# A selective-scan decoder layer on one core: products of B two units ahead in three buffers, a softplus factor in a shared tile

## The chip, the cores and the metric

The kernel runs on one core of one Trainium2 chip. A core has PE (TensorE, matrix products), DVE (VectorE), ACT (ScalarE), POOL (GpSimd) and SP (SyncE, which here only issues DMAs); each runs its own queue of instructions in order and waits on semaphores for the others. The metric is device microseconds of one execution. Before the change the median of 7 runs is 1651.39 us (1644.49 to 1654.64).

## The reference

The layer takes x of shape (4, 512, 512), four batches of 512 tokens, and adds three blocks in turn, each behind a layer norm.

1. A selective state-space block (Mamba), with 1024 channels and 16 states. Cut to what matters:

```
delta = softplus(dt_proj(dt) + bias)
h     = h * exp(delta * A) + (delta * u) * B      # for every token in turn, channel and state
y     = sum over the states of h * C
out   = out_proj((y + u * D) * silu(z))
```

2. An expert-like block with two "smooth-quantised" int8 products per batch.
3. A mixture of 16 experts with the two best chosen per token, and a shared expert.

## The kernel before

**Units.** The recurrence is done for one batch after the other. A batch has 8 chunks `c` of 128 channels; a chunk has 8 units `n`. A unit holds 2 x 32 channels with 4 of the 16 states on 128 partitions, over 512 tokens: a tile of 128 x 1024. There are 4 x 8 x 8 = 256 units. In this text scans and products are counted 0 to 255 over all batches, and chunks 0 to 31. A unit takes these steps:

- decays, two ScalarE exponentials `da` (L724) into PSUM, two buffers;
- the product of B, `bu` = B row x (delta u), on POOL (L726), two buffers in SBUF;
- the scan `da = scan(da, bu)` on VectorE (L733), which runs the recurrence along the tokens in place;
- the output `h` = da x C row on VectorE (L739);
- after four units, PE sums the states into the bank `py` (L751, `state_sums`).

**What a unit needs.** `delta(b, c)` makes a chunk's softplus: one PE product (L668), activations on ScalarE (L680 to L693: absolute value, relu, exponential, 1 + e in a tile `sp_w`, that less 1, and the logarithm in place in `sp_w`, with a table load), then on POOL a subtraction, two additions and a product with u (L695 to L701) and a memset of the first column (L703). The result is the tile `dd` (delta and delta u), two buffers. `spread(b, c, p)` then copies half a chunk's `dd` to all state rows by two DMAs on SP (L711), into `rep`, three buffers: units 0, 1, 4, 5 of a chunk read its half `p` = 0, units 2, 3, 6, 7 its half `p` = 1. The rows of B and C, `bc`, are loaded per batch in four groups (`scan_bc`, L656), one buffer each.

**The order of the work.** Nothing is reordered later: what the Python program writes is the order in each queue. `scan_batch` writes, for each unit: the decays and the product of the *next* unit (`unit_inputs`), state sums where due, other work, the scan, other work, the output, then the copies and loads that are due, other work. The "other work" (`more`) is taken from generators, one step at a time: softplus chains of coming chunks (`deltas`), the projections, convolution and gates of the next batch (`fronts`), and the second and third block of the batch before with the first group of experts (`backs`, `routed`). A generator yields what its next step needs, and `Pace` holds a running estimate of when each engine and tile will be free. A step is written if no engine it uses is estimated more than `BEHIND` later than VectorE, and its inputs no more than `SLACK`. For POOL these are 500 and -300 ns.

A half's spread is queued in `copies` (half 1 of the next chunk at unit 5, half 0 of the chunk behind it at unit 7) and written when its softplus is estimated ready. Where it isn't, it is forced, its chain's steps written out at once: half 0 after unit 6, half 1 after unit 7 of the chunk before. The B and C rows of the next batch are loaded in the last chunk after unit 4 (groups 0 and 1) and unit 7 (groups 2 and 3).

**The tail.** After the last scan come the back part of batch 3 (projection L806, quantised products, routing), what is left of the first group's expert tiles (steps L1505 to L1561: an indirect load of tokens and one of weights by POOL, transposes L400, products L1538 and L1553), then the second group of experts and the weighted sums (L1301, L1311).

Of the kernel before, what the change touches and what calls it, by code (L numbers as in the profile page):

```python
# [8 lines left out]
F32 = mybir.dt.float32  # L9
BF16 = mybir.dt.bfloat16  # L10
F16 = mybir.dt.float16
U32 = mybir.dt.uint32
# [7 lines left out]
P = 128  # L20
B = 4
L = 512
DM = 512
NT = L // P
NK = DM // P
DI = 1024
NC = DI // P
# [105 lines left out]
class Pace:  # L133
# [6 lines left out]
    TABLES = {"Exp": 0, "Tanh": 0, "Silu": 1, "Ln": 2}  # L140


    SLACK = {"DVE": 200, "Activation": 700, "Pool": -300, "PE": 3500, "SP": 500}
    BEHIND = {"DVE": 0, "Activation": 1500, "Pool": 500, "PE": 5000, "SP": 4000}

    def __init__(self, nc):
        self.nc, self.seen, self.table, self.queue = nc, 0, None, 0
# [95 lines left out]
def following(b, c, n):  # L243

    return (b, c + n) if c + n < NC else (b + 1, c + n - NC)
# [24 lines left out]
class Kernel:  # L270
# [388 lines left out]
    def delta(self, b, c):  # L659

        nc, sb, st = self.nc, self.sb, self.state[b]
        Z = self.bank

        first = (b, c) == (0, 0)
        ew, EW = (nc.vector, None) if first else (nc.gpsimd, POOL)
        yield PE, Z.free, lambda: "dt" in st and all(k >= (b, c) or x.over for k, x in self.deltas.items())
        pd = Z.take([P, L])
        nc.tensor.matmul(pd, self.wdt_sb[:, c * P : (c + 1) * P], st["dt"], start=True, stop=True)  # L668
        if c == NC - 1:
            del st["dt"]  # L670

        bias = self.bdt_sb[:, c : c + 1]
        e = sb.tile([P, L], F32, name="sp_e", bufs=1)
        w = sb.tile([P, L], F32, name="sp_w", bufs=1)
        r = sb.tile([P, L], F32, name="sp_r", bufs=1)
        dd = sb.tile([P, 2, L], F32, name="dd", bufs=2)
        st["dd", c] = dd
        delta, du = dd[:, 0, :], dd[:, 1, :]
        yield ACT, pd
        nc.scalar.activation(e, pd, AF.Abs, bias=bias)  # L680
        nc.scalar.activation(r, pd, AF.Relu, bias=bias)  # L681
        Z.done(pd)
        yield ACT
        nc.scalar.activation(e, e, AF.Exp, scale=-1.0)
        nc.scalar.activation(w, e, AF.Copy, bias=1.0)
        yield ACT
        if first:
            nc.vector.tensor_scalar_add(du, w, -1.0)
        else:
            nc.scalar.activation(du, w, AF.Copy, bias=-1.0)  # L690
        yield ACT, self.no_table
        self.table = True
        nc.scalar.activation(w, w, AF.Ln)  # L693
        yield du, EW
        ew.tensor_sub(e, e, du)  # L695
        yield EW
        ew.tensor_add(e, e, r)
        yield w, EW
        ew.tensor_add(delta, e, w)
        yield EW  # L700
        ew.tensor_mul(du, delta, st["u"][c])  # L701

        ew.memset(delta[:, 0:1], STOP)  # L703
# [9 lines left out]
            )  # L713
        st["rep"][c, p] = rep

    def unit_inputs(self, b, c, n):

        nc, st = self.nc, self.state[b]
        g, p = UNITS[n]
        rep = st["rep"][c, p]  # L720
        da = self.pscan.tile([P, NP, L], F32, name="da", bufs=2)
        for i in range(NP):
            q = c * NQC + p * NP + i
            nc.scalar.activation(da[:, i, :], rep[:, i, 0, :], AF.Exp, scale=self.a_sb[:, q, g : g + 1])  # L724
        bu = self.sb.tile([P, NP, L], F32, name="bu", bufs=2)
        nc.gpsimd.tensor_mul(bu, st["bc"][0, g].unsqueeze(1).to_broadcast([P, NP, L]), rep[:, :, 1, :])  # L726
        st["da"][c, n], st["bu"][c, n] = da, bu

    def unit_scan(self, b, c, n):
        st = self.state[b]  # L730
# [459 lines left out]
    def route(self, sb, G, b, xnT, gate):  # L1190

        nc = self.nc
        yield PE, xnT, gate, G.free
        pl = G.take([P, NT, P])
        for t in range(NT):
            for k in range(NK):
                nc.tensor.matmul(
                    pl[:, t, : E + 1],
                    xnT[:, k, t * P : (t + 1) * P],
                    gate[:, k, :],  # L1200
                    start=(k == 0),
                    stop=(k == NK - 1),
                )
        yield pl
        lg = pl[:, :, : E + 1]

        m = sb.tile([P, NT], F32, name="rt_m")
        nc.vector.tensor_reduce(m, lg[:, :, :E], AX.X, ALU.max, negate=True)
        p = sb.tile([P, NT, E + 1], F32, name="rt_p")
        nc.vector.tensor_add(p[:, :, :E], lg[:, :, :E], m.unsqueeze(2).to_broadcast([P, NT, E]))  # L1210
        nc.vector.tensor_scalar(p[:, :, E], lg[:, :, E], -1.0, 80.0, ALU.mult, ALU.min)
        yield ACT, p
        nc.scalar.activation(lg, p, AF.Exp)
        yield pl
        sg = sb.tile([P, NT], F32, name="sg")
        nc.vector.tensor_scalar_add(sg, lg[:, :, E], 1.0)
        nc.vector.reciprocal(sg, sg)
        nc.vector.tensor_reduce(m, lg[:, :, :E], AX.X, ALU.add)
        nc.vector.reciprocal(m, m)
        nc.vector.tensor_mul(p[:, :, :E], lg[:, :, :E], m.unsqueeze(2).to_broadcast([P, NT, E]))  # L1220
        G.done(pl)

        top = sb.tile([P, NT, 8], F32, name="rt_top")
        idx = sb.tile([P, NT, 8], U32, name="rt_idx")
        for t in range(NT):
            nc.vector.max(top[:, t, :], p[:, t, :E])
            nc.vector.max_index(idx[:, t, :], top[:, t, :], p[:, t, :E])
            if t % 2:
                yield
        nc.vector.tensor_copy(self.idf[:, b * NT : (b + 1) * NT, :], idx[:, :, 0:2])  # L1230
        nc.vector.tensor_reduce(m, top[:, :, 0:2], AX.X, ALU.add)
        nc.vector.reciprocal(m, m)
        yield POOL, m
        nc.gpsimd.tensor_mul(
            self.topw[:, b * NT : (b + 1) * NT, :], top[:, :, 0:2], m.unsqueeze(2).to_broadcast([P, NT, 2])
        )
        self.done.add(("route", b))
        return sg
# [115 lines left out]
    def sort(self, sb, G, group, fixed, pos, tok, wrow, count, first_weights, few):  # L1354
# [29 lines left out]
        nc.vector.tensor_copy(tot, pr[:, 1].rearrange("p t e -> p e t"))  # L1384
        G.done(pr)

        run = sb.tile([P, E, T], F32, name="run", bufs=1)
        nc.vector.tensor_tensor_scan(
            run.rearrange("p e t -> p (e t)"),
            keep.rearrange("p e t -> p (e t)"),  # L1390
# [194 lines left out]
    def run(self, ctx):  # L1585
# [21 lines left out]
        with tc.tile_pool(name="front", bufs=2) as fsb:  # L1607
            self.fsb = fsb
            self.first = ExitStack()
            sb = self.first.enter_context(tc.tile_pool(name="first", bufs=1))  # L1610
            self.xnT0 = sb.tile([P, NK, L], F32, name="xnT0", bufs=1)
            self.bank.add(self.pscan, "py")
            self.first_front(sb, self.bank)
            self.bank.names.remove((self.pscan, "py"))
            self.deltas, self.copies = {}, []
            for c in range(2):
                self.steps_of(0, c)
                self.skip(0, c)
            self.end(self.deltas[0, 0])
            self.spread(0, 0, 0)  # L1620
            for g in range(2, NG):
                self.scan_bc(0, g)
            self.spread(0, 0, 1)
            self.copies.append((0, 1, 0))
            self.fronts = Steps(self.pace, (w for b in range(1, B) for w in self.front(b)))
            self.unit_inputs(0, 0, 0)
            pool = ctx.enter_context(ExitStack())
            routed = Steps(self.pace, self.first_experts())
            backs = Steps(self.pace, self.backs(pool))
            backs.due = lambda slot: BACK_STEPS * (slot - NC * NU) / DUE  # L1630
            self.fronts.due = lambda slot: FRONT_STEPS * slot / DUE
            self.scan_batch(0, [Steps(self.pace, self.first_gates(sb))])
            for b in range(1, B - 1):
                self.scan_batch(b, [backs])
            assert self.fronts.over
# [59 lines left out]
    def scan_batch(self, b, beside):  # L1695

        self.started.add(b)
        for i in range(NC * NU):
# [3 lines left out]

            nb, nc = following(b, c, (n + 1) // NU)
            if nb < B:
                self.unit_inputs(nb, nc, (n + 1) % NU)

            if n == 4:
                self.state_sums(b, c, 0)
# [14 lines left out]
            if n == 5:  # L1723
                self.skip(*following(b, c, 2))
                self.copies.append((*following(b, c, 1), 1))
            if n == 7:
                self.copies.append((*following(b, c, 2), 0))
            while self.copies:
                db, dc, p = self.copies[0]
                if db < B:  # L1730
                    late = (db, dc) == following(b, c, 1) and n == NU - 2 + p or (db, dc) == (b, c)
                    if late:
                        self.end(self.deltas[db, dc], [*self.deltas.values(), self.fronts, *beside])
                    elif not self.deltas[db, dc].over or self.pace.ready(self.state[db]["dd", dc]) > self.pace.engine["DVE"]:
                        break
                    self.spread(db, dc, p)
                self.copies.pop(0)
            if b + 1 < B and c == NC - 1 and n in (4, 7):
                for g in range(2):
                    self.scan_bc(b + 1, g + (n == 7) * 2)  # L1740
            self.more(beside, 0)
# [67 lines left out]
```

## Time and profile before

| | |
|---|---|
| median of 7 runs | 1651.39 us |
| the profiled execution | 1649.16 us |
| span of its instructions | 1647.4 us |
| busy: PE, VectorE, POOL, ScalarE | 1199.6, 1196.7, 1126.6, 941.0 us |
| granted PE clock, mean | 0.853 |
| first scan to end of last | 85.6 to 1326.5 us |
| before the first scan; after the last | 85.6; 320.9 us |

Busy time is time in which an engine executes. The page's groups put instructions of one line together: line, engine, operation, what it writes and reads, count, then busy time in all, mean nanoseconds of one, and the idle time of that engine just ahead of them with what ended most of it. The answers on waits give total, number and longest. `PEld` is PE loading weights; `DVE da L733` is the scan's tile by the line that wrote it.

### The profile page before, as it was taken

To read this page: it belongs to the slowest core of one execution; us is meant where nothing else is said; L and a number is where in the kernel's file an instruction comes from. 1 tells how busy PE (TensorE), PEld (TensorE's weight loads), DVE (VectorE), ACT (ScalarE), POOL (GpSimd) and SP (SyncE) were. 2 spreads that over 40 slices of the span, in tenths; PEclk is the share of its full clock that TensorE was granted. 3 is DMA by queue.
4 is the path that set the end of the run, shared out by engine and by line. 5 is a ranking of instruction groups with operands and counts; after the bars stand their busy time and mean duration, and the time that the engine had idled before them with its cause. 6 is when DMAs were issued, how large, how long until landed. Compare 5 with 4: busy or idle time off the path is not lost. (4 is left out here: it accounts for less than half of the span.)

```text
span 1647.4 us, 15732 instructions
## 1 busy us (share of the span) xinstructions
PE 1199.6 (73%) x4552; PEld 586.7 (36%) x4552; DVE 1196.7 (73%) x1256; ACT 941.0 (57%) x1592; POOL 1126.6 (68%) x935
## 2 busy tenths in 40 slices
PE   5867877557866767898778885865666899668980
PEld 2223222112332323333423432353424447444760
DVE  4488999989867888878878898877787935453212
ACT  3386776755758779546787752667675415510330
POOL 1078899887768888667887874777787544135454
PEclk9978988778887887998988897888777999869995
DMA  6466555575244546665434768654567474268956
GB/s 203 143 177 137 130 117 110 125 187 111 78 89 93 124 125 178 163 190 132 98 85 118 175 149 277 164 143 124 145 178 200 122 263 146 87 254 277 338 195 217
DMA packets 109658, 262.22 MB, mean 159 GB/s; under 512 B 16192, under 2 KB 20416, under 8 KB 109504
## 3 DMA queue, kind: packets, MB, share of 16 engines
q1 hardware_dynamic: 93120, 204.50, 47.6%
q0 software_dynamic: 16448, 56.65, 9.9%
q8 instruction: 40, 0.66, 0.2%
q14 instruction: 50, 0.41, 0.1%
HBM read 168.55 MB, written 45.88 MB: 130 GB/s over the span
## 5 line engine op out<-in xcount | busy, mean ns | idle before, releaser
L726 POOL TENSOR_TENSOR bu<-bc,rep 128x1024 f32<-128x1024 f32 x256 | 602.6, 2360 | 178.7 <-DVE da L733 137.9
L733 DVE TENSOR_TENSOR_SCAN da<-da,bu 128x1024 f32<-128x1024 f32 x256 | 586.2, 2290 | 88.0 <-POOL bu L726 54.8
L724 ACT ACTIVATE da<-rep,a_sb 128x512 f32<-128x512 f32 x512 | 352.6, 690 | 250.7 <-DVE h L739 223.1
L739 DVE TENSOR_TENSOR h<-da,bc 128x1024 f32<-128x1024 f32 x256 | 312.1, 1219 | 18.5 <-PE py L751 8.2
L751 PE MATMUL py<-h,sel 128*32 128x512 f32 x1024 | 162.8, 677 | 45.6 <-DVE h L739 45.6
L1263 POOL DMA_INDIRECT wx<-in_wexp,wrow x62 | 63.5, 1025 | 87.4 <-PE bank L1553 35.4
L502 POOL TENSOR_TENSOR u<-u,tap 128x511 f32<-128x511 f32 (+2 forms) x72 | 91.3, 1268 | 16.2 <-ACT tap L498 13.9
L446 PE MATMUL bank_a<-xnT,win 128*128 128x512 f32 x176 | 93.4, 680 | 8.4 <-ACT tap L498 5.6
L446 PE MATMUL bank_g<-xnT,win 128*128 128x512 f32 x184 | 90.2, 636 | 7.6 <-ACT tap L498 4.2
L751 PEld LDWEIGHTS py<-h,sel 128*32 128x32 f32 x1024 | 31.8, 117 | 155.0 <-issue 81.0
L1507 POOL DMA_INDIRECT xs<-xn_d,tok x62 | 64.5, 1041 | 20.6 <-issue 17.7
L446 PE MATMUL bank_b<-xnT,win 128*128 128x512 f32 x120 | 60.8, 653 | 12.9 <-ACT sp_r L681 10.8
L446 PEld LDWEIGHTS bank_a<-xnT,win 128*128 128x128 f32 x176 | 37.9, 223 | 59.2 <-issue 47.9
L446 PEld LDWEIGHTS bank_g<-xnT,win 128*128 128x128 f32 x184 | 36.3, 205 | 59.9 <-issue 43.8
L411 DVE SCALAR_TENSOR_TENSOR hs<-hs,bank 128x128 f32<-128x128 f32 x24 | 6.8, 285 | 64.8 <-ACT hs L1544 48.7
L1538 PE MATMUL bank<-xT,wx 128*128 128x128 f32 x384 | 48.4, 283 | 1.9 <-ACT xT L1529 1.4
L695 POOL TENSOR_TENSOR sp_e<-sp_e,dd 128x512 f32<-128x512 f32 x31 | 39.5, 1274 | 14.3 <-ACT dd L690 14.1
L1301 POOL DMA_INDIRECT yg<-y_d,pos x32 | 32.7, 1023 | 24.0 <-DMA y_d<-ys 9.7
L1538 PEld LDWEIGHTS bank<-xT,wx 128*128 128x128 f32 x384 | 46.3, 198 | 5.4 <-issue 3.3
L1311 DVE SCALAR_TENSOR_TENSOR xr<-yg,topw,xr 128x512 f32<-128x512 f32 x32 | 23.6, 749 | 29.6 <-DMA yg<-y_d,pos 29.2
L806 PE MATMUL bank_g<-wout,u 128*128 128x512 f32 x64 | 34.6, 699 | 11.1 <-ACT tap L498 6.2
L446 PEld LDWEIGHTS bank_b<-xnT,win 128*128 128x128 f32 x120 | 24.7, 213 | 48.5 <-issue 30.3
(434 smaller groups left out, 2407.4 us busy)
## 6 DMA issues: line engine op xcount, KB each, us to landing
rep<-dd SPq DMA_DIRECT2D x128, 512.0 KB
win<-in_win SPq DMA_DIRECT2D x64, 256.0 KB
x<-xr SPq DMA_DIRECT2D x48, 256.0 KB
xr<-x SPq DMA_DIRECT2D x48, 256.0 KB
y_d<-ys SPq DMA_DIRECT2D x48, 256.0 KB
bc<-rows_d SPq DMA_DIRECT2D x32, 256.0 KB
gz_d<-gz SPq DMA_DIRECT2D x32, 256.0 KB
gzl<-gz_d SPq DMA_DIRECT2D x32, 256.0 KB
```

Source lines behind the costliest of these rows:

```text
L446: nc.tensor.matmul(pj, win[:, k, :], xnT[:, k, :], start=(k == 0), stop=(k == NK - 1))
L502: nc.gpsimd.tensor_add(u[:, j:], u[:, j:], v[j][:, j:])
L695: ew.tensor_sub(e, e, du)
L724: nc.scalar.activation(da[:, i, :], rep[:, i, 0, :], AF.Exp, scale=self.a_sb[:, q, g : g + 1])
L726: nc.gpsimd.tensor_mul(bu, st["bc"][0, g].unsqueeze(1).to_broadcast([P, NP, L]), rep[:, :, 1, :])
L733: self.nc.vector.tensor_tensor_scan(daf, daf, buf, 0.0, ALU.mult, ALU.add)
L739: self.nc.vector.tensor_mul(h, st["da"].pop((c, n)), st["bc"][1, g].unsqueeze(1).to_broadcast([P, NP, L]))
L751: nc.tensor.matmul(py[q * CH : (q + 1) * CH, :], self.sel, st["h"][c, g, q // NP][:, q % NP, :], start=False, stop=(g == NG - 1),)
L806: nc.tensor.matmul(po[t], st["u"][c][:, t * P : (t + 1) * P], wout[c], start=(c == part[0]), stop=(c == part[-1]),)
L1263: nc.gpsimd.indirect_dma_start(out=ws[s], out_offset=None, in_=self.wexp, in_offset=bass.IndirectOffsetOnAxis(ap=wrow[:, s : s + 1], axis= ...
L1507: nc.gpsimd.indirect_dma_start(out=xs[s], out_offset=None, in_=xn_d, in_offset=bass.IndirectOffsetOnAxis(ap=tok[:, s : s + 1], axis=0), bo ...
L1538: nc.tensor.matmul(ph[:, i, :], w[:, o : o + P], xT[:, k, :], start=(k == 0), stop=(k == NK - 1))
```

## The change

The product is taken out of `unit_inputs` and made two units ahead, with a third `bu` buffer; the decays stay one unit ahead. `sp_w` is gone: 1 + e and its logarithm now stand in the delta half of `dd`, and the steps that follow wait for `dd`. POOL's `SLACK` goes to 2500 and its `BEHIND` to 3500. Half 0 is queued at unit 6 instead of 7 and forced after unit 5 instead of 6; half 1 as before. Groups 0 and 1 of the next batch's rows are loaded after unit 3 instead of 4. Some tiles of the routing have one buffer, and the experts' sort runs its scan in place in `keep`. The packs of state sums are as they were.

```diff
-    SLACK = {"DVE": 200, "Activation": 700, "Pool": -300, "PE": 3500, "SP": 500}
-    BEHIND = {"DVE": 0, "Activation": 1500, "Pool": 500, "PE": 5000, "SP": 4000}
+    SLACK = {"DVE": 200, "Activation": 700, "Pool": 2500, "PE": 3500, "SP": 500}
+    BEHIND = {"DVE": 0, "Activation": 1500, "Pool": 3500, "PE": 5000, "SP": 4000}
...
-        w = sb.tile([P, L], F32, name="sp_w", bufs=1)
...
+        w = delta
...
-        yield du, EW
+        yield dd, EW
         ew.tensor_sub(e, e, du)
         yield EW
         ew.tensor_add(e, e, r)
-        yield w, EW
+        yield dd, EW
         ew.tensor_add(delta, e, w)
...
-    def unit_inputs(self, b, c, n):
+    def unit_decays(self, b, c, n):
...
-        bu = self.sb.tile([P, NP, L], F32, name="bu", bufs=2)
-        nc.gpsimd.tensor_mul(bu, st["bc"][0, g].unsqueeze(1).to_broadcast([P, NP, L]), rep[:, :, 1, :])
-        st["da"][c, n], st["bu"][c, n] = da, bu
+        st["da"][c, n] = da
+
+    def unit_products(self, b, c, n):
+
+        nc, st = self.nc, self.state[b]
+        g, p = UNITS[n]
+        bu = self.sb.tile([P, NP, L], F32, name="bu", bufs=3)
+        nc.gpsimd.tensor_mul(
+            bu, st["bc"][0, g].unsqueeze(1).to_broadcast([P, NP, L]), st["rep"][c, p][:, :, 1, :]
+        )
+        st["bu"][c, n] = bu
...
-        run = sb.tile([P, E, T], F32, name="run", bufs=1)
+        run = keep
...
-            self.unit_inputs(0, 0, 0)
+            self.unit_decays(0, 0, 0)
+            for n in range(2):
+                self.unit_products(0, 0, n)
...
             if nb < B:
-                self.unit_inputs(nb, nc, (n + 1) % NU)
+                self.unit_decays(nb, nc, (n + 1) % NU)
+            nb, nc = following(b, c, (n + 2) // NU)
+            if nb < B:
+                self.unit_products(nb, nc, (n + 2) % NU)
...
-            if n == 7:
+            if n == 6:
                 self.copies.append((*following(b, c, 2), 0))
...
-                    late = (db, dc) == following(b, c, 1) and n == NU - 2 + p or (db, dc) == (b, c)
+                    late = (db, dc) == following(b, c, 1) and n == NU - 3 + 2 * p or (db, dc) == (b, c)
...
-            if b + 1 < B and c == NC - 1 and n in (4, 7):
+            if b + 1 < B and c == NC - 1 and n in (3, 7):
+                while ("rows", b + 1) not in self.done:
+                    self.fronts.go()
```

The tiles `rt_m`, `rt_p`, `sg`, `rt_top` and `rt_idx` of the routing get `bufs=1`.

More of the change, by code (lines that the diff above doesn't have):

```diff
@@ L1205, in route @@
         lg = pl[:, :, : E + 1]
-        m = sb.tile([P, NT], F32, name="rt_m")
+        m = sb.tile([P, NT], F32, name="rt_m", bufs=1)
         nc.vector.tensor_reduce(m, lg[:, :, :E], AX.X, ALU.max, negate=True)
-        p = sb.tile([P, NT, E + 1], F32, name="rt_p")
+        p = sb.tile([P, NT, E + 1], F32, name="rt_p", bufs=1)
         nc.vector.tensor_add(p[:, :, :E], lg[:, :, :E], m.unsqueeze(2).to_broadcast([P, NT, E]))
@@ L1214, in route @@
         yield pl
-        sg = sb.tile([P, NT], F32, name="sg")
+        sg = sb.tile([P, NT], F32, name="sg", bufs=1)
         nc.vector.tensor_scalar_add(sg, lg[:, :, E], 1.0)
@@ L1221, in route @@
         G.done(pl)
-        top = sb.tile([P, NT, 8], F32, name="rt_top")
-        idx = sb.tile([P, NT, 8], U32, name="rt_idx")
+        top = sb.tile([P, NT, 8], F32, name="rt_top", bufs=1)
+        idx = sb.tile([P, NT, 8], U32, name="rt_idx", bufs=1)
         for t in range(NT):
```

## The prediction

> **What bounds the kernel now.** I read the page's groups first, then the waits of VectorE and POOL, then the busy time by stage, then the timeline of one long wait. The page's four costliest groups: the product, the scan, the decays and the output of a unit.
> ```profile
> L726 POOL TENSOR_TENSOR bu<-bc,rep 128x1024 f32<-128x1024 f32 x256 | 602.6, 2360 | 178.7 <-DVE da L733 137.9
> L733 DVE TENSOR_TENSOR_SCAN da<-da,bu 128x1024 f32<-128x1024 f32 x256 | 586.2, 2290 | 88.0 <-POOL bu L726 54.8
> L724 ACT ACTIVATE da<-rep,a_sb 128x512 f32<-128x512 f32 x512 | 352.6, 690 | 250.7 <-DVE h L739 223.1
> L739 DVE TENSOR_TENSOR h<-da,bc 128x1024 f32<-128x1024 f32 x256 | 312.1, 1219 | 18.5 <-PE py L751 8.2
> ```
> A unit costs VectorE 2.29 + 1.22 = 3.51 us, POOL 2.36, ScalarE 2 x 0.69. ScalarE and POOL mostly stand waiting for VectorE (223.1 and 137.9 us): VectorE sets the pace. Busy time by stage (batch 0, 1, 2, 3 of the scans; the first part of the tail; the rest of it):
> ```profile
> core 0: us, PE busy (x) PEld busy (x) DVE busy (x) ACT busy (x) POOL busy (x), PEclk, DMA share, GB/s
> 85.60:348.10 262.50, 180.48 (x524) 62.21 (x524) 238.50 (x160) 193.07 (x304) 234.75 (x166) 0.81 0.59 131
> 348.10:663.50 315.40, 222.53 (x788) 99.35 (x788) 260.99 (x234) 225.47 (x379) 252.29 (x202) 0.84 0.51 125
> 663.50:987.40 323.90, 268.21 (x915) 118.12 (x916) 270.52 (x250) 215.90 (x358) 249.10 (x186) 0.90 0.55 137
> 987.40:1326.50 339.10, 235.34 (x1004) 127.29 (x1003) 277.26 (x292) 188.60 (x324) 238.85 (x199) 0.82 0.59 166
> 1326.50:1440.00 113.50, 99.49 (x531) 65.95 (x529) 44.35 (x103) 47.71 (x101) 41.65 (x53) 0.96 0.48 171
> ```
> The 256 scans run from 85.6 to 1326.5, one each (1326.5 - 85.6) / 255 = 4.87 us. In these 1240.9 us VectorE is busy 238.5 + 261.0 + 270.5 + 277.3 = 1047.3 and idle 193.6. That idle time is all that any change to the coupling can win. The waits (total, times, longest) say how much of it stands at a scan:
> ```profile
> POOL bu L726 <- DVE da L733: 137.9, 77, 8.5
> ...
> DVE da L733 <- POOL bu L726: 54.8, 27, 11.5
> ...
> POOL bu L726 <- DMA rep<-dd: 35.0, 5, 20.7
> ...
> DVE da L733 <- ACT da L724: 32.5, 22, 4.4
> ```
> 54.8 us wait for a product, 32.5 for a decay. Read one by one in VectorE's timeline, two of the 27 product waits are long: 11.1 before the first scan, and 11.5 at scan 88 (the first of chunk 11, counting chunks over the batches). The other 25 are 54.8 - 11.1 - 11.5 = 32.2 us, mostly of 0.4 to 2.3 us. Scan 88 in the timeline:
> ```profile
> 454.68 0.10 POOL L703 MEMSET dd<- 128x1 f32 x1
> 454.81 7.62 SPq L711 DMA_DIRECT2D rep<-dd  x4
> ...
> 461.71 0.69 ACT L724 ACTIVATE da<-rep,a_sb 128x512 f32<-128x512 f32 x1 [9.34 <-DMA rep<-dd]
> ...
> 463.69 4.65 POOL L726 TENSOR_TENSOR bu<-bc,rep 128x1024 f32<-128x1024 f32 x2 [8.91 <-DMA rep<-dd]
> ...
> 466.07 2.30 DVE L733 TENSOR_TENSOR_SCAN da<-da,bu 128x1024 f32<-128x1024 f32 x1 [11.47 <-POOL bu L726]
> ```
> Here it is not POOL's load: the softplus chain ended (L703) just ahead of the chunk's first product, and its spread took 9.0 us from there to landing (454.7 to 463.7); the decays waited for the same spread. (Columns: start, duration, what, and in brackets the idle time before it and what ended it.)
>
> **The change, part by part.** Both programs have the same instructions on every engine; only places, buffers and waits differ.
>
> *Products two ahead, three buffers (L726, new L732).* Product k used to wait for the end of scan k-2 and stood in POOL's queue at the head of unit k-1; now it waits for scan k-3 and stands at the head of unit k-2. So the queue looks as before, with product k in the place of product k-1. At each of the 25 short waits, product k-1 had ended 3.6 to 8.3 us before VectorE came free, so its place is early enough. What is late next is the decay, still one unit ahead in two PSUM tiles: at six of the 25 (scans 9, 110, 117, 176, 206, 235) its activation ended 1.6, 1.1, 0.3, 0.2, 0.5 and 2.7 us after VectorE came free, together 6.4. That leaves 32.2 - 6.4 = 25.8. One unit of lead is given once per crowded stretch. In batch 0 (POOL busy 234.8 of 262.5) the short waits add up to 9.1 us, at 599 to 614 us to 3.5, at 1220 to 1240 to 5.6; if POOL never recovered its lead within a stretch, each would keep what exceeds 3.5: 5.6 + 0 + 2.1 = 7.7. POOL's 137.9 us of waiting for scans lies between them, so I take half, 4: gain **22**, between 18 and 26.
>
> *Spreads and the tight chunks.* The spread is allowed one unit earlier and is forced after unit 5 instead of 6, its product stands one unit earlier too. Room decides: from the start of the last product m ahead of a softplus chain, POOL needs what stands up to the memset, 9.0 for the spread, and 2.36; VectorE asks for product 8c after one output (1.2) and (8c - m + 2) units of 4.87, as product m starts at the end of scan m-3. Over the 31 chunks, with the order of POOL's instructions and the durations of the page, this gives before (one unit less) a large deficit only at chunk 11, 10.0 us (measured 11.5), and of -1 to -3 at two chunks where no long wait was seen. After, chunk 11's chain stands one product earlier: 5.0 + 9.0 + 2.4 = 16.4 against 1.2 + 4 x 4.87 = 20.7: the wait goes. I take **9** of 11.5, between one unit (4.9) and all. In the new order the chain of chunk 16 stands directly ahead of its first product, with layer-norm scales among it: 10.0 + 9.0 + 2.4 = 21.4 against 1.2 + 3 x 4.87 = 15.8, a new wait of **5.5**, between 0 and 9 (if all of the landing is exposed). Chunks 1, 11, 21 and 30 keep 4 to 6 us of room, all others over 6. The first wait of 11.1 stays: nothing stands ahead of it.
>
> *The softplus factor in dd.* Saves a tile. The planner now writes the subtraction after the logarithm (a table load of 1.28 and 0.63): the chain starts up to 1.9 us later. Room of 4 us or more hides it; at chunk 16 it is within my bounds.
>
> *POOL's limits in the planner (SLACK, BEHIND), rows of B and C at unit 3.* No cost by themselves, but they move work. Counting what stands after the last scan's work on each engine: VectorE 472 to 476 instructions, PE 1322 to 1336, POOL's expert loads 48 to 50 of each kind: two tiles of the first group of experts move into the tail. There PE is busy 99.5 of 113.5 us (1326.5 to 1440). A tile is eight L1538 matmuls of 0.29, one L1553 of 0.69 and four transposes of 0.27, so 4.1 us on PE, 8.2 for two. They can fill the 14 idle us, or stand in front of the last batch's projections: **+4**, between 0 and 8.2. VectorE loses four of a tile's swishes, 0.285 each, from the scans: -1. The B and C rows are loaded two units ahead of their first product, as before, but for groups 2 and 3, where two of three units remain (9.7 us): nothing, as VectorE has two more products by then.
>
> *Single buffers in the routing, keep in place of run.* Tiles that are allocated once per batch, and one scan in place: nothing; no instruction waits for more.
>
> *What I can't read.* ScalarE's decays had time to catch up while VectorE waited for POOL; the new order also shifts PE's banks. VectorE's idle time but for the product waits inside the stretch is 193.6 - 43.7 = 150 us; a tenth of it either way, -15 to +15, is an estimate of what such shifts can do. I take **+4**, on the side of the six scans above, where ScalarE was nearly late.
>
> Sum: -22 - 9 + 5.5 + 4 - 1 + 4 = -18.5. The profiled execution took 1649.2 (span 1647.4), 2.2 under the median of 1651.4, so 1630.7 for it, and 1633 beside the median.
>
> **A rule against it.** By the trace's answer for its line the shortest scan took 2.267 us, the median 2.289, the longest 2.299, whether or not a product ran beside it. The Trainium skill, "SBUF — State Buffer", section "SBUF: two separate sides", says that VectorE and GpSimd hold a shared port pair exclusively, the loser blocked for a whole instruction, when a VectorE operation has two SBUF inputs. Here the scan's and the output's first operand is da, in PSUM, so the rule would not bite; if it did, a product could lose up to the scan's 2.29 us, POOL would need 4.65 of 4.87 us for products alone, and the gain of 22 would be 0. The rows show no such loss, and the sum stays.
>
> **The rivals.**
> 1. *The decay takes over.* For it: 32.5 us of waits already, and decays are not made earlier. Against: ScalarE waits 223.1 us for VectorE. If every short wait turned into one for a decay, only chunk 11 would be won: 1651.4 - 9 + 5.5 + 4 - 1 = 1651; with half of them, 1640. Chance 0.17.
> 2. *More than the sum.* The waits that follow from late POOL work beside the scans (taps, scales) shrink too, the tail takes the tiles for nothing: -26 - 11.5 + 0 + 0 - 1 - 4 = -42, so 1609. Chance 0.13.
> 3. *Slower: the spread's landing.* POOL now meets the spread a unit earlier, and a POOL that stands at it holds up what is behind it in its queue. The place is the first product of chunks 1, 11, 16, 21 and 30, with 5.6, 4.3, -5.5, 5.6 and 5.6 us of room at a landing of 9.0. Without chunk 16's wait the sum wins 18.5 + 5.5 = 24. A landing longer by x costs 5x + 5.5 - 4.3 - 3 x 5.6 = 5x - 15.6, so it decides from x = 7.9, a landing of 17 us. At 20 us (x = 11) it costs 39.4: 1651.4 - 24 + 39.4 = 1667. For it: the DMA engines are 51 to 59% busy here, and SP's queue is in order. Against: chunk 11's landing of 9.0 was in such traffic. Chance 0.14.
> 4. *It doesn't get ahead.* POOL is too full in batch 0 (89%) for a lead: 9.1 less, so 1642. Part of the forecast's range.
>
> **Numbers.** Forecast (1618 to 1645) 0.56, rivals 1, 2, 3 as above. I call 1633 the likeliest. The range reaches to rival 2's end and past the no-gain end of rival 1: 1609 to 1657; above it lies rival 3. 0.3%, about what a measurement can tell from no change, is 5 us: 1646.4 to 1656.4. Faster: 0.56 + 0.13 + a fifth of rival 1 = 0.72; same: the rest of rival 1 = 0.14; slower 0.14.
>
> **What would show it.** Right: the scan's wait for bu near 23 us (11.1 of it the first), no long wait at scan 88, one of about 5 at scan 128; the scans' stretch near 1218 instead of 1240.9; the tail after the last scan 321 to 330. Wrong: a scan's wait for da well over 40; POOL's wait for rep well over 35 with the scans late behind it; a tail over 335.

## The result, and the profile after

The change makes the kernel slower. After: 1675.78 us (median of 18 runs, 1666.89 to 1687.88); before, on the same chip: 1651.45 (46 runs, 1641.87 to 1658.0). The ratio is 1.0158, interval [1.014, 1.0176]. Forecast were 1633 us and a range up to 1657.

The page's groups of the kernel after, the four that were read before:

```profile
L732 POOL TENSOR_TENSOR bu<-bc,rep 128x1024 f32<-128x1024 f32 x256 | 602.0, 2360 | 196.0 <-DVE da L741 94.5
L741 DVE TENSOR_TENSOR_SCAN da<-da,bu 128x1024 f32<-128x1024 f32 x256 | 586.0, 2289 | 73.6 <-ACT da L724 41.2
L724 ACT ACTIVATE da<-rep,a_sb 128x512 f32<-128x512 f32 x512 | 352.0, 689 | 199.7 <-DVE h L747 163.8
L747 DVE TENSOR_TENSOR h<-da,bc 128x1024 f32<-128x1024 f32 x256 | 312.4, 1220 | 19.3 <-PE py L759 9.1
```

Read alone, they look like the forecast. None of the four takes longer; the scan's idle time falls from 88.0 to 73.6, and it now waits most for a decay, no longer for a product. Its product waits in the answer on waits:

```profile
POOL bu L732 <- DVE da L741: 94.5, 45, 9.2
POOL bu L732 <- DMA rep<-dd: 70.5, 16, 8.4
...
DVE da L741 <- ACT da L724: 41.2, 29, 5.2
...
DVE xn L1170 <- PE bank_g L1147: 29.6, 7, 9.1
DVE da L741 <- POOL bu L732: 28.9, 11, 11.5
```

Product waits went from 54.8 us in 27 to 28.9 in 11 (one of them the 11.5 before the first scan). Three of these lines grew: `da <- ACT` (32.5 to 41.2), POOL's wait for a spread (35.0 in 5, one of them the 20.7 before the first scan, to 70.5 in 16) and L1170's wait for PE, which is read below. The busy time by stage shows where the loss stands (batches 0 to 3 of the scans, then the tail):

```profile
core 0: us, PE busy (x) PEld busy (x) DVE busy (x) ACT busy (x) POOL busy (x), PEclk, DMA share, GB/s
87.30:349.90 262.60, 188.15 (x512) 60.62 (x512) 237.97 (x160) 189.28 (x298) 230.62 (x158) 0.79 0.56 129
349.90:659.60 309.70, 228.71 (x796) 103.61 (x796) 259.16 (x230) 223.00 (x376) 248.03 (x200) 0.81 0.52 127
659.60:1013.90 354.30, 287.17 (x919) 127.79 (x920) 274.80 (x252) 220.87 (x367) 258.47 (x196) 0.87 0.50 127
1013.90:1353.70 339.80, 230.33 (x969) 119.21 (x968) 279.97 (x288) 186.87 (x321) 232.96 (x195) 0.79 0.58 162
1353.70:1683.60 329.90, 245.43 (x1228) 162.85 (x1226) 111.68 (x277) 89.88 (x190) 145.12 (x162) 0.85 0.64 225
```

Against before, batch 0 is +0.1 us, batch 1 -5.7, **batch 2 +30.4**, batch 3 +0.7, the tail +9.0, and the first scan starts 1.7 later: 36.2 together, which is the difference of the spans (1683.6 - 1647.4). These are two single executions, and the one after took 1685.3 us, 9.5 above its median, with the lowest mean clock of its runs (0.831); the medians differ by 24.3. Batch 2's length doesn't come from that: e2 and e10 below have 354.5 and 354.2 us there, in executions 0.2 and 2.6 us from their medians. In batch 2 VectorE has 252 records against 250 and is busy 4.3 us longer (274.8 and 270.5); the other 26 us are idle time.

To see what it stands at, I added up the idle time ahead of each VectorE instruction in the scans' stretch, by what stands behind it: a scan that a product or a decay released, an output `h` or the gated sum, or other work (anything else):

| us | stretch | tail | scan, product | scan, decay | output | other work |
|---|---|---|---|---|---|---|
| before | 1240.9 | 320.9 | 44.3 | 32.6 | 28.7 | 88.0 |
| after | 1266.4 | 329.9 | 17.5 | 41.5 | 26.6 | **125.8** |

(After the change two scans that another step of POOL released, 3.2 us together, stand in no column.) The product waits fell by 27, nearly as forecast; 9 came back at the decays, and 38 at instructions that are not part of the recurrence at all, 24 of these in batch 2. One step of the third block makes 24 of the 38: L1170, which was L1162, waits in the scans' stretch 5.5 us for PE before and 29.2 after. Before:

```profile
DVE xn L1162 <- PE bank_g L1139: 4.8, 3, 2.4
...
DVE xn L1162 <- PE bank_a L1139: 0.7, 1, 0.7
```

After:

```profile
DVE xn L1170 <- PE bank_g L1147: 24.0, 6, 9.1
...
DVE xn L1170 <- PE bank_a L1147: 5.2, 1, 5.2
```

The first big piece, in VectorE's timeline of the kernel after (start, duration, what, and the idle time before it with what ended it):

```profile
706.69 0.69 DVE L1170 SCALAR_TENSOR_TENSOR xn<-xn,bank_g 128x512 f32<-128x512 f32 x1 [7.23 <-PE bank_g L1147]
...
716.23 1.22 DVE L747 TENSOR_TENSOR h<-da,bc 128x1024 f32<-128x1024 f32 x1
719.37 0.75 DVE L1185 SCALAR_TENSOR_TENSOR xr<-bank_a,sg,xr 128x512 f32<-128x512 f32 x1 [1.92 <-DMA xr<-x]
722.48 0.75 DVE L1185 SCALAR_TENSOR_TENSOR xr<-bank_g,sg,xr 128x512 f32<-128x512 f32 x1 [2.35 <-PE bank_g L1179]
725.91 0.75 DVE L1185 SCALAR_TENSOR_TENSOR xr<-bank_b,sg,xr 128x512 f32<-128x512 f32 x1 [2.68 <-PE bank_b L1179]
729.34 0.75 DVE L1185 SCALAR_TENSOR_TENSOR xr<-bank_a,sg,xr 128x512 f32<-128x512 f32 x1 [2.68 <-PE bank_a L1179]
730.01 2.29 DVE L741 TENSOR_TENSOR_SCAN da<-da,bu 128x1024 f32<-128x1024 f32 x1
```

These are steps of the third block (the shared expert, of the batch before), and they stand in VectorE's queue in front of scans 137 and 139. The first waits 7.2 us for PE. The four additions are each written as soon as a product of PE is estimated ready; PE delivers one every 3.4 us, and VectorE cannot pass them to scan 139. Measured from scan 128, the kernel after is 4.1 us ahead of before at scan 136 and 9.9 behind at scan 140.

The second kind of piece, late in the same batch, in the timelines of ScalarE, PE and VectorE:

```profile
984.50 1.41 ACT L724 ACTIVATE da<-rep,a_sb 128x512 f32<-128x512 f32 x2
...
989.77 2.29 DVE L741 TENSOR_TENSOR_SCAN da<-da,bu 128x1024 f32<-128x1024 f32 x1
...
991.15 5.37 PE L1155 MATMUL bank_g<-xnT,ws 128*128 128x512 f32 x8 [2.89 <-DMA ws<-in_wexp]
...
996.55 0.60 ACT L1162 ACTIVATE xn<-bank_g 128x512 f32<-128x512 f32 x1 [10.65 <-PE bank_g L1155]
997.05 2.74 ACT L724 ACTIVATE da<-rep,a_sb 128x512 f32<-128x512 f32 x4
998.56 2.30 DVE L741 TENSOR_TENSOR_SCAN da<-da,bu 128x1024 f32<-128x1024 f32 x1 [5.24 <-ACT da L724]
```

Read it upwards. Scan 189 waited 5.2 us for its decays; these stood in ScalarE's queue behind L1162, a step of the third block, which stood 10.65 us for a product that PE had begun only at 991.15, after 2.89 us of waiting for its weights. By its busy share ScalarE has time to spare (221 of 354 us), and still it is late: what counts is what stands at the head of its queue.

PE was also slower at this place. The eight matmuls of L1155 took 5.37 us where the eight of L1147 right behind them took 3.60; the granted clock reads 0.51 of full speed from 992 to 994 us and 0.76 from 994 to 997. Over batch 2 it reads 0.87 against 0.90 before, and PE is busy 287.2 us with 919 matmuls against 268.2 with 915. No run holds the clock and changes the order, so how much of batch 2's loss the lower clock makes stays open.

### The profile page after: what moved, and what is told of

It is laid out like the page before. It is cut to its first block, busy times and chain, and to the rows that moved or that the text cites. A ratio compares the mean times of both kernels' runs of the same rounds, so it can differ in the third digit from the quotient of the medians.

```text
span 1683.6 us, 15692 instructions
## 1 busy us (share of the span) xinstructions
PE 1240.4 (74%) x4552; PEld 598.1 (36%) x4552; DVE 1202.5 (71%) x1256; ACT 939.6 (56%) x1592; POOL 1123.5 (67%) x935
## 5 line engine op out<-in xcount | busy, mean ns | idle before, releaser
L732 POOL TENSOR_TENSOR bu<-bc,rep 128x1024 f32<-128x1024 f32 x256 | 602.0, 2360 | 196.0 <-DVE da L741 94.5
L741 DVE TENSOR_TENSOR_SCAN da<-da,bu 128x1024 f32<-128x1024 f32 x256 | 586.0, 2289 | 73.6 <-ACT da L724 41.2
L747 DVE TENSOR_TENSOR h<-da,bc 128x1024 f32<-128x1024 f32 x256 | 312.4, 1220 | 19.3 <-PE py L759 9.1
L759 PE MATMUL py<-h,sel 128*32 128x512 f32 x1024 | 174.2, 691 | 59.3 <-DVE h L747 59.3
L1271 POOL DMA_INDIRECT wx<-in_wexp,wrow x62 | 63.0, 1016 | 115.5 <-PE bank_b L1561 36.2
L446 PE MATMUL bank_b<-xnT,win 128*128 128x512 f32 x160 | 91.8, 726 | 12.8 <-ACT sp_r L681 11.1
L446 PE MATMUL bank_a<-xnT,win 128*128 128x512 f32 x144 | 73.1, 655 | 7.5 <-DMA win<-in_win 3.8
L446 PEld LDWEIGHTS bank_b<-xnT,win 128*128 128x128 f32 x160 | 36.8, 240 | 67.5 <-issue 46.9
L1546 PE MATMUL bank<-xT,wx 128*128 128x128 f32 x352 | 43.2, 277 | 5.6 <-issue 4.2
L446 PEld LDWEIGHTS bank_a<-xnT,win 128*128 128x128 f32 x144 | 29.6, 213 | 47.3 <-issue 38.0
L1546 PEld LDWEIGHTS bank<-xT,wx 128*128 128x128 f32 x352 | 41.2, 192 | 7.7 <-issue 5.9
L755 PE MATMUL py<-u,skip 128*128 128x512 f32 x64 | 39.2, 698 | 6.0 <-DVE u L781 6.0
L1155 PE MATMUL bank_a<-xnT,ws 128*128 128x512 f32 x56 | 33.8, 760 | 12.1 <-DMA ws<-in_wexp 9.5
```

The source lines that it names most:

```text
L446: nc.tensor.matmul(pj, win[:, k, :], xnT[:, k, :], start=(k == 0), stop=(k == NK - 1))
L741: self.nc.vector.tensor_tensor_scan(daf, daf, buf, 0.0, ALU.mult, ALU.add)
L747: self.nc.vector.tensor_mul(h, st["da"].pop((c, n)), st["bc"][1, g].unsqueeze(1).to_broadcast([P, NP, L]))
L759: nc.tensor.matmul(py[q * CH : (q + 1) * CH, :], self.sel, st["h"][c, g, q // NP][:, q % NP, :], start=False, stop=(g == NG - 1),)
L1271: nc.gpsimd.indirect_dma_start(out=ws[s], out_offset=None, in_=self.wexp, in_offset=bass.IndirectOffsetOnAxis(ap=wrow[:, s : s + 1], axis= ...
L1546: nc.tensor.matmul(ph[:, i, :], w[:, o : o + P], xT[:, k, :], start=(k == 0), stop=(k == NK - 1))
```

## The experiments

The experiments ran on three chips, on which the median of the kernel before is 1635 to 1636 us, less than on the chip of the result. Every ratio is against the kernel before on the experiment's own chip; stage times of two runs are often of two chips, and of one execution each. Two runs of the unchanged kernels anchor the rest.

**e5, e9: before and after again, there.** No edit.

> The kernel before, unchanged, for a profile on the same chip as the next three (in the first four runs the kernel before took 1636 us against 1651 elsewhere, so stretches of the program should be compared on one chip). Every theory: within 0.5% of the kernel before; its scans' stretch near 1241 us, and the difference between chips in the part after the last scan.

> The changed kernel, unchanged, on one chip with the next three. Every theory: ratio 1.012 to 1.020. Beside run 2 (the same order, products one ahead, 1.0212) it gives what the lead is worth in the new order: 0.3 to 0.8% if the lead helps there, 0 if it never helps.

Before: one run of 1633.45 beside a median of 1635.79. After: 1662.29, ratio 1.0154 [1.0113, 1.0195]; batches 263.9, 308.2, 357.7 and 339.8, in an execution 9 us above the median. The loss belongs to the program: batch 2 is again 30 us longer (327.7 in e5).

### The lead by itself, and the order by itself

**e1: before's order, products two ahead.** The planner's yes and no answers were recorded from before and replayed, so that softplus chains, spreads, layer norms and expert steps stand where they stood. A product is written up to two ahead, but not ahead of its spread, which stays in its old place.

```diff
-        if not self.over and self.pace.clear(self.wait, ...):
+        if not self.over and PLAN.say(lambda: self.pace.clear(self.wait, ...)):
...
+            while self.made < min(self.slot + 3, B * NC * NU):
+                pb, pi = divmod(self.made, NC * NU)
+                pc, pn = divmod(pi, NU)
+                if (pc, UNITS[pn][1]) not in self.state[pb]["rep"]:
+                    break
+                self.unit_products(pb, pc, pn)
+                self.made += 1
```

> All of the change's products, buffers and tiles, with every other instruction in the place that the kernel before gave it: the planner's answers of before are written into the program as a list (POOL's limits, the spreads' and the rows' places are those of before too). Theory 'order' (the planner's new order of the other work costs the time, the products' lead by itself wins what was forecast): 1620 to 1635 us, ratio 0.98 to 0.99, the scan's waits for bu near 15 to 20 us. Rival 'lead' (POOL that meets the spreads a unit earlier holds up its queue): 1665 to 1685. Rival 'nothing gained' (the decay takes over): 1645 to 1655.

1633.79 us, ratio 0.9993 [0.998, 1.0005]: nothing. Of the waits of VectorE:

```profile
DVE da L800 <- ACT da L783: 53.8, 32, 9.4
DVE da L800 <- POOL bu L791: 28.4, 5, 11.4
```

Only 5 product waits are left (22.8 of the 28.4 us are the first scan and scan 88), and the decays took over most of what was won: their waits went from 34.8 in e5 to 53.8, 19 us, while the product waits inside the stretch fell from 41.0 to 17.1, 24 us. Waits at other work rose too, from 88.7 to 95.2. Some of the waits for a decay are large: scan 243 stands 9.4 us, against 4.3 in e5. This is rival 1's mechanism, and nearly its full size.

**e2: after's order, products one ahead, two buffers.** The same device with after's answers.

```diff
-        bu = self.sb.tile([P, NP, L], F32, name="bu", bufs=3)
+        bu = self.sb.tile([P, NP, L], F32, name="bu", bufs=2)
...
-            nb, nc = following(b, c, (n + 2) // NU)
             if nb < B:
-                self.unit_products(nb, nc, (n + 2) % NU)
+                self.unit_products(nb, nc, (n + 1) % NU)
```

> The counterpart: every instruction but the products in the place that the changed kernel gives it, the products one unit ahead in two buffers as before. Theory 'order': slower than the changed kernel, 1690 to 1705, since it has the new order and not the lead. Rival 'lead': back to 1645 to 1655.

1672.1 us, ratio 1.0212 [1.0193, 1.0231]. The whole loss is there with the lead gone. Batch 2 takes 354.5 us, and the same L1170 step waits the same 7.2 us. The lead is worth something in this order: product waits inside the stretch are 64.6 us here and 17.5 after, decay waits 12.8 and 41.5, and e9 is about 0.6% faster (the intervals just touch). With the order held, it is not the lead that costs; that the earlier products are among the edits from which the planner laid this order is another matter.

**e8: e1 with chunk 11's chain and first spread one unit earlier.** This takes the long wait at scan 88 by itself.

```diff
-                    late = (db, dc) == following(b, c, 1) and n == NU - 2 + p or (db, dc) == (b, c)
+                    late = ... or (db, dc, p, n) == (1, 3, 0, 5) and c == 2
```

> Run 1 (old order, products two ahead), with the softplus chain and the first spread of chunk 11 written one unit earlier, after unit 85 instead of 86; nothing else moves but twelve lines of POOL's and ScalarE's queues and the spread's place on SP. The wait of 11.5 us at scan 88 was left standing in run 1. If the spread's lateness made it: 4 to 10 us less than run 1, ratio 0.993 to 0.997. If the chain can't start earlier since its inputs are late: 0.998 to 1.001.

1641.79 us, ratio 1.0037 [1.0023, 1.0052], slower than e1. The wait at scan 88 went, and another took its place one unit earlier:

```profile
456.32 0.10 POOL L762 MEMSET dd<- 128x1 f32 x1
...
465.48 2.34 POOL L791 TENSOR_TENSOR bu<-bc,rep 128x1024 f32<-128x1024 f32 x1 [7.85 <-DMA rep<-dd]
...
469.65 0.23 POOL L997 TENSOR_SCALAR s<-s 128x4 f32<-128x4 f32 x1
469.91 0.18 DVE L999 RECIPROCAL rs<-s 128x4 f32<-128x4 f32 x1 [15.58 <-POOL s L997]
```

POOL now meets the spread early, with a product that nobody needs yet, and waits 7.85 us. Behind it in its queue stand four small steps of the quantisation, 1.7 us together, and VectorE had already been given the reciprocal that needs them: 15.6 us of standing in place of 11.5. A product made early is harmless to the scans and can still be in the way. This is the mechanism of rival 3, at a landing of 9 us (456.4 to 465.5) and not of 17.

**e10: after's order, scans ahead of the other work.** From batch 1 on each scan is written before the first turn of the other work.

```diff
+            first = self.slot >= NC * NU
+            if first:
+                self.unit_scan(b, c, n)
             self.more(beside, 3500)
-            self.unit_scan(b, c, n)
+            if not first:
+                self.unit_scan(b, c, n)
```

> The changed kernel's order (written into the program as a list), but from batch 1 on each scan stands ahead of the other work that its unit writes before it: only VectorE's queue changes, by 39 scans. If VectorE loses its time by standing at other work whose inputs are late, with a scan that is ready behind it, these scans fill it: 5 to 20 us faster than the changed kernel, ratio 1.002 to 1.012. If the outputs, and with them decays and sums, come as much later: no faster, 1.012 to 1.025.

1664.65 us, ratio 1.0177 [1.0119, 1.0235]: no gain. The other work's waits fell from 127.8 (e9) to 110.1, the scans' waits for decays rose from 43.3 to 54.4, and outputs took 3 more. A scan that is let ahead tends to find its decay late. But the run tests less than was meant: in its trace 29 scans stand earlier in VectorE's queue, not 39, and in batch 2's stretch scan 137 still stands behind the L1170 step (7.3 us of waiting) and scan 139 behind two of the four additions. From scan 136 to 140 it loses 11.7 us against before, where the kernel after loses 13.9. So it doesn't show what this stretch would take with its scans ahead.

### POOL's limits in the planner

**e3: after with the old limits; e4: before with the new ones.**

```diff
-    SLACK = {"DVE": 200, "Activation": 700, "Pool": 2500, "PE": 3500, "SP": 500}
-    BEHIND = {"DVE": 0, "Activation": 1500, "Pool": 3500, "PE": 5000, "SP": 4000}
+    SLACK = {"DVE": 200, "Activation": 700, "Pool": -300, "PE": 3500, "SP": 500}
+    BEHIND = {"DVE": 0, "Activation": 1500, "Pool": 500, "PE": 5000, "SP": 4000}
```

> The changed kernel with POOL's SLACK of -300 and BEHIND of 500 of before; the planner lays out the rest anew. If the limits' new values by themselves made the bad order: 1625 to 1645. If the earlier products and spreads upset the planner whatever the limits (the old limits fit a POOL that is one unit ahead, so they hold POOL's work back more): 1670 to 1700, with more work left for the tail.

> The kernel before with POOL's SLACK of 2500 and BEHIND of 3500, nothing else. If these values make the bad order: 1670 to 1690. If they only make up for products that stand a unit earlier: POOL is let in up to 3 us later than before, so products come late; 1650 to 1665.

e3 is 1681.74 us, ratio 1.0280 [1.0251, 1.0309]; e4 is 1665.62, ratio 1.0187 [1.0162, 1.0212]. Either step away from its partner costs. They cost in different places: e3 has batch 2 at 326.6 and pays with a tail of 336.7; e4 has a short tail, 298.2, and pays in batch 0 (273.8) and batch 3 (350.2).

**e13: after, old limits in batch 2 alone; e14: old limits up to the end of batch 2.**

```diff
-            if self.engine[e] > base + self.BEHIND[e] or ready > base + self.SLACK[e]:
+            slack, behind = self.SLACK[e], self.BEHIND[e]
+            if e == "Pool" and 128 <= self.slot < 192:
+                slack, behind = -300, 500
+            if self.engine[e] > base + behind or ready > base + slack:
...
+            self.pace.slot = self.slot
```

(e14 has `self.slot < 192`.)

> The kernel after, but with POOL's old limits in the planner (-300 and 500 ns) while the scans of batch 2 are written (units 128 to 191); outside of them the new limits. Batch 2 lasted 323.9 us in the kernel before, 354.3 after, and 326.6 in the kernel after with the old limits throughout. If the new limits in that batch make its loss, through work written too early behind POOL's layer norm, batch 2 falls to about 327 and the whole, unless the tail takes tiles, to 1636 x 1.0155 - 27, a ratio near 0.999. If the loss is only a matter of which order was drawn, batch 2 lands anywhere between 325 and 355, or what it wins comes back in batch 3 and the tail, and the ratio stays between 1.006 and 1.028 like those of the other draws.

> The kernel after, but with POOL's old limits up to the end of batch 2's scans and the new ones from batch 3 on. With the old limits throughout batches 0 to 2 lasted 262.0, 321.0 and 326.6 us, batch 3 345.9 and the tail 336.7; the new limits gave 339.8 and 312 on these chips. If stretches can be put together, this would be 88 + 262 + 321 + 327 + 340 + 312 = 1650, a ratio near 1.010. If work that is not written in one stretch comes back in the next, batch 3 and the tail stay at about 346 and 337 and the ratio stays near 1.028.

e13 is 1649.37 us, ratio 1.0084 [1.0053, 1.0115], against 1.0154 [1.0113, 1.0195] in e9 (the intervals just touch). Its batches are 263.1, 309.4, 338.2 and 340.1 and its tail 311.3: all within 1.5 us of e9 but for batch 2, which is 16.1 us shorter than on the first chip (19.5 shorter than in e9's slower execution).

```profile
657.90:996.10 338.20, 278.21 (x917) 126.98 (x920) 272.37 (x252) 221.52 (x366) 257.60 (x196) 0.88 0.53 133
```

As many records of VectorE and nearly as many of PE in 338 instead of 354 us. Of the 16 us, 10 are decay waits (16.7 to 6.8 in this batch; the one at scan 189 is gone) and 3 stand at outputs. What stayed are the waits at other work (54.1 us after, 54.7 here, 30.5 before) and the stretch of scans 136 to 140 (13.8 us lost there, 13.9 after). So of batch 2's 30 us about **16 go with the old limits in that batch** and **14 remain**: 9.8 by scan 140, the rest up to the batch's end. If the limits had made the whole loss of this batch, it would have come down to about 327 us and the ratio to 0.999; 338 and 1.0084 lie where the expectation put a mere other draw of the order, so it isn't shown that the limits' values matter and not that the order was drawn anew. That the L1170 and L1185 steps make the 14 is read from the timelines; they stand there in after, e2 and e13 alike, and no run takes them away. Against e5 the span is 15.8 us longer: batch 2 +10.5, the tail +9.1, batch 3 +3.5, batch 1 -7.5, the start -0.6 and batch 0 +0.8.

e14 is 1660.23, ratio 1.0148 [1.0114, 1.0183]. Batch 2 is 331.6 and the tail 293.8, and batch 3 grew from 339.8 to 368.6. Work that one stretch doesn't take comes back in the next.

### A touch of the planner that has nothing to do with the change

`HOP` is the planner's estimate, in ns, of the time from one engine's end to another's start. It changes no instruction, only what is estimated ready, and so the order.

```diff
-    HOP = 120
+    HOP = 130
```

> The kernel before, with one number of the planner's estimate touched that has nothing to do with the products: 130 ns instead of 120 from an instruction's end to its reader's start (HOP). The programs do the same instructions in another order. Theory 'settled order' (the order of before is one of the better ones that this planner gives, and any change to its input costs): ratio 1.01 to 1.03. Rival 'guilty lead' (orders with products two ahead are worse, others are not): 0.997 to 1.005.

> The changed kernel with the same touch, 130 for 120. 'Settled order': another draw, anywhere between 1.00 and 1.035 of the kernel before. 'Guilty lead': near the changed kernel, 1.012 to 1.020.

> A second draw for the planner of before: 110 ns for 120 in HOP. 'Settled order': 1.01 to 1.03 as with 130. If 130 was an unlucky draw: 0.997 to 1.008.

> A third draw for the planner with the change. 'Settled order': 1.00 to 1.035, with no relation to the changed kernel's 1.016; if orders with the lead are as good on average as those of the touched planner of before, the three (this, run 7 and the changed kernel) lie about its two.

> The kernel before with the planner's estimate of a semaphore hop at 125 instead of 120 ns, half of the smaller step already tried (130 gave 1.019, 110 gave 1.011). If the order of the kernel before is a settled good one, any touch loses 1 to 2%: 1.010 to 1.020. If small touches cost in proportion to the step, about 1.009 or less. If it is neither, within 0.3% of 1.

> The kernel after with the planner's estimate of a hop at 125 instead of 120 ns. Draws of the kernel after so far: 1.0154 to 1.016, 1.022 at 130, 1.006 at 110. If the order is what decides, this is one more draw between 1.005 and 1.025; if the kernel after has a loss of its own beside the order, at or above 1.015.

| HOP | before's program | after's program |
|---|---|---|
| 110 | 1.0110 [1.0067, 1.0154] (e11) | 1.0059 [1.0041, 1.0076] (e12) |
| 120 | 1 | 1.0154 [1.0113, 1.0195] (e9) |
| 125 | 1.0048 [1.0031, 1.0065] (e15) | 1.0166 [1.0133, 1.0199] (e16) |
| 130 | 1.0192 [1.0167, 1.0216] (e6) | 1.0222 [1.0195, 1.0248] (e7) |

Ten nanoseconds in an estimate cost the kernel before 1.9%, more than the change costs. All three touches of before made it slower, and at 110 the changed kernel comes out below the unchanged one (their intervals overlap). At 120 the kernel before has the lowest time of its column, so a comparison there alone puts any new order at a disadvantage. The mean of the column is 1.009 before and 1.015 after, with a spread inside each column of 0.016 to 0.019.

## Why the prediction was wrong, step by step

**What failed: "What I can't read".** The prediction put the re-laid order at +4 us, with -15 to +15 as an estimate from a tenth of VectorE's idle time. It measured about +36: e2 has the new order without the lead and is 36.0 us over its own before (1672.1 - 1636.1). The error behind the number is that every step was costed as a local edit in an order that otherwise stands. With a planner that asks at each step what is estimated ready, one earlier product or another limit moves all that follows, and a touch of 10 ns by itself costs 1.9 or 1.1% (e6, e11). Nothing in the profile of before could give the sign, but the size could have been known as open: the instructions' order in both programs could be seen to differ nearly throughout, and 88 us of VectorE's idle time stood at other work.

**"POOL's limits", "no cost by themselves".** The term gave them only the tail's tiles. The new limits alone put the kernel before 29.5 us over its own before (e4: 1665.62 - 1636.12), and without them in batch 2 the kernel after has 16 us less there (e13). Whether their values do this or any new order would, these runs don't tell apart.

**"Products two ahead", -22.** The mechanism was read rightly and the price was not. Short product waits went as forecast, but the allowance for late decays was 6.4 us, taken from six scans where ScalarE was seen to be late; in the old order decays take 19 of the 24 us and other work the rest (e1; the time is the same). One of the 25 waits read as short, at scan 217, is 5.69 us; after the change it is 1.38. ScalarE and POOL "mostly stand waiting for VectorE" was the argument against rival 1. It counts idle time; a decay's lateness is set by the step in front of it on ScalarE, which waits for PE or for POOL. Rival 1 had the mechanism, though not the total, since the order's price was not in it.

**"Spreads and the tight chunks", -9 and +5.5.** The wait at scan 88 fell from 11.47 to 2.50 us in the kernel after, 9.0 as forecast; chunk 16's new wait came at scan 128 with 3.19 instead of 5.5, and two of about that size that I had not seen came at scans 16 (2.69) and 240 (4.85, the first of chunk 30, for which 5.6 us of room were reckoned). Whether 9 us of wait are 9 us of time is another matter: e8 took that wait alone and lost 0.4%.

**The tail, +4.** +9.0 on the chip of the result and +10.1 in the repeats (312.3 in e9, 302.2 in e5), PE busy 10.5 us more in it. The two tiles are there (16 more matmuls of L1546, two more of L1561), but the larger part is one that the term did not have: 13 more matmuls of the shared expert's second product (L1179, before L1171) run after the last scan. PE is busy with that line 26.2 us in the tail, against 19.3 before. That the size lay near the upper bound of 8.2 is luck.

**Rules and costs that held.** No operation of a unit got dearer on POOL, VectorE or ScalarE: the product's mean is 2360 ns in both, the scan's 2290 and 2289, and the scan's shortest and longest are 2.264 and 2.299 us with products at new places beside it. So the port rule that was weighed has no price here, as the rows of before had it. PE's state sums did get longer, 677 to 691 ns in the mean, at a mean granted clock of 0.853 and 0.831. The softplus factor in `dd`, the single buffers and `keep` were not run alone; e1 has them all, with the lead, in before's order and takes before's time, so a cost of theirs could only be one that the lead pays for.

**Rival 3** had the sign and, near enough, the time (1667 against 1675.8), by luck, for its cause is not the one here. POOL's wait for spreads in the scans' stretch did rise, from 14.3 us in 4 to 70.5 in 16, but the scans' product waits fell. Of those over 1.5 us inside the stretch three stand behind such a wait (scans 16, 128 and 240, 10.7 us together), and of VectorE's waits over 1.5 us for the quantisation's scales none does. Its mechanism is real in e8, by a way that the prediction did not name, through the quantisation's scales to VectorE.

**What stays open.** Why batch 2's decays come late with the new limits is only argued: POOL's steps stand earlier, and PE, the weight loads and ScalarE are then met in another order. What the lower granted clock in batch 2 costs was not tried. And four draws of each kernel can't tell whether the change is worth a little less than nothing by itself or nothing: 1.009 and 1.015 with such spreads are not apart. What is shown is that the loss stands with the order and not with the lead in it (e2), that the lead wins nothing in before's order (e1), and that the loss is of a size that an unrelated touch makes too.

## What to carry to other kernels

When an order is laid out by a planner from estimates, cost a change in two parts, the edit in the old order and the re-laying, and measure both: replay the old order with the edit for the first, and jitter an unrelated constant for the second; a gain smaller than the jitter isn't yet a gain. Before giving one input of a step more lead, ask when its other input arrives, and look for that at the head of the queue of the engine that makes it, not at that engine's share of busy time. An instruction made early on an in-order engine moves its wait forward to where other things stand behind it.

## What the runs showed that was not expected

The same program took 1651.4 us on one chip and 1635 to 1636 where the experiments ran (medians), and the difference is not spread evenly. In one execution of each, the scans' stretch is 1240.9 and 1243.5 us (e5), the tail 320.9 and 302.2. In the tail the DMA engines moved 227 GB/s on the one and 241 on the other, with PE busy 234.9 and 230.5 us. What in the tail makes the difference was not tried.
